# A Fourier layer: half-array forward transform, output in parts of 64 channels

## The chip, the cores and the metric

The kernel runs on one core of one Trainium2 chip. The metric is the device time of one execution in microseconds, as the median of several runs. A core has a matrix engine (TensorE, PE in the profile, with its weight loads as PEld), three elementwise engines (VectorE as DVE, ScalarE as ACT, GpSimd as POOL) and a queue from which transfers are issued (SyncE, SP). Each engine works through its own list of instructions in order, and waits at an instruction until what it needs is there.

## The reference

Four layers follow each other on a tensor of 4 batches, 96 channels and 4096 tokens: a state-space layer, a convolution layer, an attention layer with a quantized feed-forward part, and a Fourier layer with a second such feed-forward part. The change is in the Fourier layer alone:

```
h = einsum('bnc,hc->bnh', layernorm(t), w1)            # 96 -> 192 channels
h = relu(bn(h, bn1...))
X = fft(h, axis=1, norm='ortho')                       # over the 4096 tokens, per channel
xr = relu(X.real * rd - X.imag * id + rb)              # rd, id: one number per channel
xi = relu(X.imag * rd + X.real * id + ib)
y = ifft(xr + 1j * xi, axis=1, norm='ortho').real
t = t + bn(einsum('bnh,ch->bnc', y, w2), bn2...)       # 192 -> 96 channels
```

## The kernel before

A transform over 4096 tokens is done as 128 x 32: token = 32 a + n. The real input is transformed over a (128 points, of which frequencies 0 to 64 are kept), turned by twiddle factors, transformed over the 32 values of n, treated by the ReLU part, and brought back in the opposite order. Everything is float32; a matmul is recorded as two instructions, which the profile counts separately.

The unit of work is an iteration `j` of the loop in `fourier`: a group of G = 6 times 4 channels. There are 32 iterations, 8 per batch; four make one half (96 of the 192 channels) of a batch. The order of instructions on PE, DVE, ACT and POOL is written by hand (`manual_schedule`: program order is queue order), and it is a software pipeline. The transfers on SP are ordered by the scheduler. One iteration `j` emits, in this order:

- `over_n1(j)`: six matmuls over 128 points into `s_ps` (L1390); two DVE products `p` with the twiddles (L1394); two POOL additions that make the real and the imaginary part `f` on 128 partitions (L1402).
- `norm1`, `norm2` (layer norm of the next batch, in iterations where the half is even, for three batches) or `w1`, called by `turn` (the first projection of the next batch, in iterations where the half is odd). `norm1` needs a `misc` buffer on PE, a DVE instruction writes `h` (L1357), ACT squares it; `norm2` is a matmul, two ACT instructions and a POOL product (L1367). `w1` is two matmuls and two ACT instructions that write `hh` (L1378).
- `fold(j-2)`: ACT ReLU on half of `av` (L1436), then on DVE in this order `zz`, `z`, `zz`, `z` (L1441, L1444), and an ACT negation of a part of `zz` (L1447). The two `zz` instructions read two tensors that lie in SBUF.
- `over_k1` and `w2` for two blocks of four token columns, of the half that was finished four iterations before: four matmuls of 128 x 96 weights (L1494), an ACT copy `ys` (L1496), one matmul with the second projection (L1505), one DVE addition into `t` (L1509 or L1511).
- `over_n2(j-1)`: four matmuls of 128 x 128 weights and 390 columns (L1411 to L1414), a DVE product `ec` (L1417), twelve ACT instructions into `av` (L1426), a POOL addition and a POOL subtraction (L1429, L1430).
- `over_k2(j-3)`: twelve matmuls (L1459, L1460) into two PSUM buffers, and an ACT copy `bt` of each (L1461).

Every fourth iteration `row64` sends the row of frequency 64 through a small DRAM buffer into `bt`. The PSUM buffers matter: tag `m` (`misc`) has two and serves `norm1`, `norm2`, `w1`, `over_k1`, `w2` and `row64` in turn; tag `i1` has two and serves `over_k2`. The inverse matrix for a block (`gt`, 256 KB) comes from DRAM, with two buffers; near the end the whole matrix is fetched into free `hh` buffers.

The two blocks are called the first and the second block below. The order of the middle of an iteration, shortened:

```python
over_n1(j)
norm1(b, a, sq)                 # or turn(2)
fold(j - 2)
over_k1(*blocks[0], kept)
norm2(a - MB, sq)
over_n2(j - 1)
norm1(b, a + MB, sq)
w2(*blocks[0], kept)
over_k1(*blocks[1], kept)
over_k2(j - 3)
norm2(a, sq)                    # or turn
w2(*blocks[1], kept)
```

Of the kernel before, what the change touches and what calls it, by code (L numbers as in the profile page):

```python
# [9 lines left out]
F32 = mybir.dt.float32  # L10
# [92 lines left out]
class Net:  # L103
# [717 lines left out]
    def consts2(self, wk, small):  # L821
# [28 lines left out]
        self.dft2 = load("dft2", [128, 3 * 128])  # L850
# [54 lines left out]
        self.a_w2 = pool.tile([C, 2, C], F32, name="a_w2s")  # L905
        for half in range(2):
            ps = small(C, C)
            nc.tensor.matmul(ps, araw[:, half * C : (half + 1) * C], gain, start=True, stop=True)
            nc.vector.tensor_copy(self.a_w2[:, half], ps)
# [425 lines left out]
    def fourier(self, dram, t, h):  # L1335
# [3 lines left out]
        units = [(b, half) for b in range(B) for half in range(2)]  # L1339
        its = [(u, g) for u in range(len(units)) for g in range(0, CG, G)]  # L1340
        with ExitStack() as ctx:
# [3 lines left out]
            nbs, bc, bs = (self.dft2[:, k * 128 : (k + 1) * 128] for k in range(3))  # L1345
# [23 lines left out]
            def w1(b, n):  # L1369

                if n == 0:
                    for half in range(2):
                        hh[2 * b + half] = wk.tile([N1, CG, N2, 4], F32, name="hh", tag="hh", bufs=3)
                ps = misc(N1)[:, : 4 * C].rearrange("p (n c) -> p n c", n=2)
                for d in range(2):
                    nc.tensor.matmul(ps[:, d, :], h[:, n + d :: N2], self.a_w1, start=True, stop=True)  # L1376
                for half in range(2):
                    nc.scalar.activation(  # L1378
                        hh[2 * b + half][:, :, n : n + 2, :].rearrange("p g n c -> p n g c"),
                        ps[:, :, half * C : (half + 1) * C].rearrange("p n (g c) -> p n g c", c=4),  # L1380
                        AF.Relu,
                    )

            def over_n1(i):

                u, g = its[i]
                ps = pln.tile([128, 2, MB], F32, name="s1_ps", tag="s1")
                for d in range(G):
                    a = d % 3 * 2 * K1
                    nc.tensor.matmul(ps[:, d // 3, a : a + 2 * K1], hh[u][:, g + d], self.dft1, start=True, stop=True)  # L1390
                pp = []
                for k in range(2):
                    p = wk.tile([128, G, 2, K1], F32, name=f"p{k}", tag=f"p{k}")
                    nc.vector.tensor_mul(  # L1394
                        p.rearrange("p (a g) r k -> p a g (r k)", a=2),
                        ps[:, :, : 6 * K1].rearrange("p a (g k) -> p a g k", g=3),
                        self.twid[:, k : k + 1, None, :].to_broadcast([128, 2, 3, 2 * K1]),
                    )
                    pp.append(p)
                f[i] = wk.tile([128, 2, G, K1], F32, name="f", tag="f", bufs=2)  # L1400
                for r in range(2):
                    nc.gpsimd.tensor_add(f[i][:, r], pp[0][:, :, r, :], pp[1][:, :, 1 - r, :])  # L1402

            def over_n2(i):

                u, g = its[i]
                cg = units[u][1] * CG + g
                fr, fi = (f[i][:, r].rearrange("p g k -> p (g k)") for r in range(2))
                f.pop(i)
                xr, xi = (pln.tile([128, MB], F32, name=f"x{r}_ps", tag=f"x{r}")[:, : G * K1] for r in "ri")  # L1410
                nc.tensor.matmul(xi, bc, fi, start=True, stop=False)  # L1411
                nc.tensor.matmul(xi, nbs, fr, start=False, stop=True)
                nc.tensor.matmul(xr, bc, fr, start=True, stop=False)
                nc.tensor.matmul(xr, bs, fi, start=False, stop=True)  # L1414
# [17 lines left out]
            def fold(i):  # L1432

                u, g = its[i]
                v = av.pop(i)
                nc.scalar.activation(v[:, 1:3], v[:, 1:3], AF.Relu)  # L1436
                z = zz[i] = wk.tile([128, G, 3, K1 - 1], F32, name="zz", tag="zz", bufs=2)
                if g == 0:
                    z64[u] = wk.tile([128, 2, CG], F32, name="z64", tag="z64", bufs=2)
                for k, (one, two, op) in enumerate(((0, 2, ALU.add), (3, 1, ALU.subtract))):  # L1440
                    nc.vector.scalar_tensor_tensor(  # L1441
                        z[:, :, 1 + k], v[:, one, :, : K1 - 1], 0.0, v[:, two, :, : K1 - 1], ALU.max, op
                    )
                    nc.vector.scalar_tensor_tensor(  # L1444
                        z64[u][:, k, g : g + G], v[:, one, :, K1 - 1], 0.0, v[:, two, :, K1 - 1], ALU.max, op
                    )
                nc.scalar.mul(z[:, :, 0], z[:, :, 2], -1.0)  # L1447

            def over_k2(i):

                u, g = its[i]
                z = zz.pop(i)
                if g == 0:
                    bt[u] = wk.tile([N1, N2, C], F32, name="bt", tag="bt", bufs=2)
                for e in range(0, G, 3):
                    ps = pln.tile([N1, 4, 128], F32, name="i1_ps", tag="i1", bufs=2)[:, :3]
                    for d in range(3):
# [3 lines left out]
                    nc.scalar.copy(  # L1461
                        bt[u].rearrange("p n (g c) -> p g n c", c=4)[:, g + e : g + e + 3],
                        ps.rearrange("p g (n c) -> p g n c", c=4),
                    )

            def row64(u):
                ps = misc(CG)[:, :128]
                for k in range(2):
                    nc.tensor.matmul(ps, z64[u][:, k], self.dft64[:, k], start=k == 0, stop=k == 1)
                r = wk.tile([CG, N2, 4], F32, name="r64", tag="r64", bufs=2)  # L1470
                nc.scalar.copy(r, ps.rearrange("p (n c) -> p n c", c=4))
                d = dram.tile([1, N2 * C], F32, name="d64", tag="d64", bufs=2)
                nc.sync.dma_start(d.rearrange("o (n g c) -> g (o n) c", n=N2, c=4), r)
                nc.sync.dma_start(bt[u][64:65].rearrange("p n c -> p (n c)"), d)
# [3 lines left out]
            def fetch(k):  # L1478

                g = wk.tile([N1, CG, N2, 4], F32, name="hh", tag="hh", bufs=3)  # L1480
                g = g.rearrange("p g n c -> p (g n c)")[:, : N2 // 2 * N1].rearrange("p (n a) -> p n a", n=N2 // 2)
# [4 lines left out]
            def over_k1(u, n, kept):  # L1486
                if n in late:
                    gt = late[n]
                else:
                    gt = wk.tile([N1, 4, N1], F32, name="gt", tag="gt", bufs=2)  # L1490
                    nc.sync.dma_start(gt, ins["idft"][:, n : n + 4])
                ps = misc(C).rearrange("p (n a) -> p n a", n=4)
                for d in range(4):
                    nc.tensor.matmul(ps[:, d], bt[u][:, n + d], gt[:, d], start=True, stop=True)  # L1494
                kept[u, n] = wk.tile([C, MB], F32, name="ys", tag="ys", bufs=2)
                nc.scalar.copy(kept[u, n], ps.rearrange("p n a -> p (n a)"))  # L1496

            def w2(u, n, kept):

                b, half = units[u]  # L1500
                if u < len(units) - 1:
                    ps = misc(C)
                else:
                    ps = pln.tile([N1, 4, 128], F32, name="i1_ps", tag="i1", bufs=2)[:C].rearrange("p n a -> p (n a)")
                nc.tensor.matmul(ps, self.a_w2[:, half, :], kept.pop((u, n)), start=True, stop=True)  # L1505
                ps = ps.rearrange("p (n a) -> p n a", n=4)
                td = ft[b][:, n : n + 4]
                if half == 0:
                    nc.vector.scalar_tensor_tensor(td, ps, self.b2, td, ALU.add, ALU.add)  # L1509
                else:  # L1510
                    nc.vector.tensor_add(td, td, ps)  # L1511

            engines = {mybir.EngineType.PE, mybir.EngineType.DVE, mybir.EngineType.Activation, mybir.EngineType.Pool}
            with tc.manual_schedule(engines=engines):
# [3 lines left out]
                for j in range(len(its) + 4):  # L1518
                    ub, k = divmod(j - 2 * PER, PER)
                    blocks = [(ub, n) for n in (8 * k, 8 * k + 4)] if 0 <= ub < len(units) else []  # L1520
# [30 lines left out]
                    if blocks:  # L1551
                        w2(*blocks[0], kept)
                        over_k1(*blocks[1], kept)
# [6 lines left out]
                    if (j - 6) % PER == 0 and 0 <= (j - 6) // PER < len(units):  # L1560
                        row64((j - 6) // PER)
                    turn(len(tokens))
                    if blocks:
# [4 lines left out]
                last = [(len(units) - 1, n) for n in range(0, N2, 4)]  # L1568
# [31 lines left out]
def _constants():  # L1600
# [9 lines left out]
    th = 2 * np.pi * np.outer(np.repeat(np.arange(N2), 4), k1) / L  # L1610
# [4 lines left out]
    eye = np.eye(4)  # L1615
    bc, bs = np.kron(np.cos(th), eye), np.kron(np.sin(th), eye)
    dft2 = np.concatenate([-bs, bc, bs], 1)

    th = np.pi * np.outer(2 * m + 1, m) / N2
    dft64 = np.stack([np.kron(np.cos(th), eye), np.kron(-np.sin(th), eye)], 1)  # L1620
# [12 lines left out]
        "dft2": dft2.astype(f32),  # L1633
        "dft64": dft64.astype(f32),
# [18 lines left out]
def _lay_out(i):  # L1653
# [20 lines left out]
    for k, v in (("rd", np.diagonal(a["r"])), ("id", np.diagonal(a["i"])), ("rb", a["rb"]), ("ib", a["ib"])):  # L1674
        v128[k] = np.tile(v.reshape(48, 4).T, (32, 1))
# [56 lines left out]
```

## Time and profile before

| what | value |
|---|---|
| median of 3 runs | 3710.8 us (3705.59 to 3724.08) |
| profiled execution, its own time | 3723.78 us |
| span of the profiled execution | 3722.0 us |
| mean granted TensorE clock | 0.914 |
| PE, DVE, ACT, POOL busy | 83%, 81%, 73%, 69% |
| Fourier loop, first `over_n1` to the next layer's first matmul | 3097.04 to 3589.5 us of the span |

Times are microseconds from the start of the span. A group line gives the line of the kernel, the engine, the output and inputs, the shape (partitions x elements), the count, then busy time and mean ns of one, then idle time of the engine before these instructions and what ended it. Overlapping matmuls are recorded with their pipeline, so the mean of one matmul is longer than the step from one to the next. A window line gives, for a stretch of time, the busy time of each engine with the number of instructions.

### The profile page before, as it was taken

The numbers are of one execution on the slowest core, as the hardware profiler recorded it, in microseconds if no ns is written. First come the engines' busy times: TensorE is split into PE (matmuls) and PEld (weight loads), VectorE is DVE, ScalarE is ACT, GpSimd is POOL, SyncE is SP. The second block draws the span as 40 slices with busy tenths as digits, with TensorE's granted clock in tenths as the row PEclk, the third lists the DMA queues.
The fourth block names the chain that finished last, engine by engine and source line by source line (L and its number), as shares of the span: only waits on it lengthen the run. The fifth ranks groups of instructions, "written<-read, shape, count | busy, mean of one in ns | idle before, by whom it ended". The sixth has DMA issues, their size and how long they took to land. (4 is left out here: it accounts for less than half of the span.)

```text
span 3722.0 us, 47365 instructions
## 1 busy us (share of the span) xinstructions
PE 3098.0 (83%) x15360; PEld 1409.3 (38%) x15360; DVE 3020.9 (81%) x2966; ACT 2722.6 (73%) x5584; POOL 2567.9 (69%) x925
## 2 busy tenths in 40 slices
PE   7888788878887888888888878659798888999888
PEld 3332223222322232223222322228345436667643
DVE  5999999999999999999999999962665693444649
ACT  5888888887888887888888878641346786656557
POOL 1989988899899988998998999832001263444427
PEclk8999999989999999899999999859899998999989
DMA  7666656665666666666666666557000000011001
GB/s 186 151 162 155 170 152 161 156 169 153 160 155 169 160 153 156 172 158 152 158 171 160 148 165 160 145 149 272 12 0 1 1 1 6 24 35 47 24 12 58
DMA packets 171552, 446.36 MB, mean 120 GB/s; under 512 B 48756, under 2 KB 50750, under 8 KB 167968
## 3 DMA queue, kind: packets, MB, share of 16 engines
q1 hardware_dynamic: 171304, 443.34, 46.2%
q8 instruction: 121, 1.98, 0.2%
q14 instruction: 127, 1.04, 0.1%
HBM read 369.68 MB, written 73.50 MB: 119 GB/s over the span
## 5 line engine op out<-in xcount | busy, mean ns | idle before, releaser
L648 POOL TENSOR_TENSOR hs<-hs,crep 128x2048 f32<-128x2048 f32 x384 | 1601.7, 4187 | 224.4 <-DVE hs L643 177.2
L610 ACT ACTIVATE da<-ddb,nega 128x1024 f32<-128x1024 f32 x576 | 660.1, 1146 | 200.3 <-DMA ddb<-dd 129.1
L643 DVE TENSOR_TENSOR_SCAN hs<-da,state,rep 128x1024 f32<-128x1024 f32 x288 | 669.5, 2338 | 47.8 <-PE rep L594 28.0
L621 POOL TENSOR_TENSOR up<-udb,brep 128x1024 f32<-128x1024 f32 x192 | 453.6, 2363 | 83.3 <-DMA udb<-ud 62.2
L665 PE MATMUL y<-hs,sel_r 128*32 128x512 f32 x3072 | 462.2, 696 | 12.2 <-POOL hs L648 11.9
L599 PE MATMUL rep<-dbl,sel_b 32*128 32x512 f32 x768 | 249.9, 729 | 215.6 <-DVE hs L643 215.5
L507 ACT ACTIVATE uta<-delta,bt 128x192 f32<-128x192 f32 x1024 | 379.7, 441 | 0.0
L287 PE MATMUL ps<-n,w_x 97*64 97x512 f32 x1536 | 354.5, 604 | 12.5 <-ACT xc L411 11.8
L643 DVE TENSOR_TENSOR_SCAN hs<-da,state,u 128x1024 f32<-128x1024 f32 x144 | 338.1, 2348 | 23.7 <-PE y L665 7.8
L643 DVE TENSOR_TENSOR_SCAN hs<-dap,state,up 128x1024 f32<-128x1024 f32 x144 | 335.3, 2328 | 1.5 <-ACT dap L610 1.4
L594 PE MATMUL rep<-ident,uta 128*128 128x128 f32 x1536 | 223.0, 287 | 103.6 <-DVE hs L643 89.9
L594 PEld LDWEIGHTS rep<-ident,uta 128*128 128x128 f32 x1536 | 175.2, 146 | 248.6 <-issue 136.2
L636 DVE TENSOR_TENSOR u<-udb,rep 128x1024 f32<-128x1024 f32 x192 | 235.3, 1226 | 25.0 <-DMA udb<-ud 11.4
L643 DVE TENSOR_TENSOR_SCAN hs<-da,rep 128x1024 f32<-128x1024 f32 x96 | 218.0, 2281 | 19.5 <-PE rep L594 13.5
L610 ACT ACTIVATE dap<-ddb,nega 128x1024 f32<-128x1024 f32 x192 | 214.1, 1115 | 24.8 <-DVE hs L643 24.3
L636 DVE TENSOR_TENSOR rep<-udb,rep 128x1024 f32<-128x1024 f32 x192 | 231.8, 1207 | 0.0
L1290 POOL CAST hq<-y 128x1536 fp8e5<-128x1536 f16 x64 | 94.0, 1469 | 198.2 <-DVE y L1289 136.3
L287 PEld LDWEIGHTS ps<-n,w_x 97*64 97x64 f32 x1536 | 105.1, 137 | 259.1 <-issue 208.8
L665 PEld LDWEIGHTS y<-hs,sel_r 128*32 128x32 f32 x3072 | 73.9, 119 | 337.1 <-issue 261.7
L599 PEld LDWEIGHTS rep<-dbl,sel_b 32*128 32x128 f32 x768 | 65.8, 205 | 353.5 <-issue 299.1
L658 PE MATMUL y<-xc,dp 128*128 128x512 f32 x192 | 132.0, 778 | 31.3 <-ACT bt L463 31.3
L1157 POOL MEMSET h<- 1x4096 f32 x1 | 3.5, 3507 | 215.0 <-ACT g L1039 215.0
(287 smaller groups left out, 6291.6 us busy)
## 6 DMA issues: line engine op xcount, KB each, us to landing
udb<-ud SPq DMA_DIRECT2D x768, 128.0 KB
ddb<-dd SPq DMA_DIRECT2D x768, 128.0 KB
crep<-cd SPq DMA_DIRECT2D x512, 128.0 KB
dd<-delta SPq DMA_DIRECT2D x64, 384.0 KB
band<-in_band SPq DMA_DIRECT2D x24, 1024.0 KB
ud<-delta SPq DMA_DIRECT2D x62, 384.0 KB
brep<-cd SPq DMA_DIRECT2D x128, 128.0 KB
x<-in_x SPq DMA_DIRECT2D x32, 384.0 KB
```

What stands on the lines that cost most here:

```text
L287: nc.tensor.matmul(ps[rows], w[:, 64 * p : 64 * p + 64], rhs[:, at.start + shift : at.stop + shift], start=k == 0, stop=k == len(ws) - 1, ...
L507: nc.scalar.mul(m["uta"][:, q, :, 32 * s4 : 32 * s4 + 32].rearrange("t (p j) d -> t p j d", p=3), m["udt"][:, :, q].rearrange("t p (j d) - ...
L594: nc.tensor.transpose(x[:, q * 128 : q * 128 + 128], made[k]["uta"][:, q, 2 * h + j], self.ident)
L599: nc.tensor.matmul(x[:, at], sel_b[rows, g], made[k]["dbl"][rows, at], start=True, stop=True)
L610: nc.scalar.activation(da, made[k]["dd", h, j], AF.Exp, scale=nega[:, col : col + 1])
L621: nc.gpsimd.tensor_mul(up, made[k]["ud", p][:, j], made[k]["brep", GP])
L636: nc.vector.tensor_mul(u, made[k]["ud", h][:, j], x)
L643: nc.vector.tensor_tensor_scan(hs[:, 1:], made[k].pop(("da", t)), u, st, ALU.mult, ALU.add)
L648: nc.gpsimd.tensor_mul(hs[:, :, :T], hs[:, :, 1:], twice(made[k]["crep", g]))
L658: nc.tensor.matmul(y, dp[:, items[k][2], p], made[k]["xc"][:, p], start=True, stop=True)
L665: nc.tensor.matmul(made[k]["y", p][row : row + 32], sel_r, made[k]["hs", p, g][:, j, at], start=False, stop=True, skip_group_check=True,)
L1290: nc.gpsimd.tensor_copy(q, y2, saturate=False)
```

## The change

The forward transform over 32 points is laid out differently. The partitions of `s_ps` now hold (channel, n) in place of (n, channel), and `f` holds, for two of the four channels at a time, the real part on partitions 0 to 63 and the imaginary part on 64 to 127. Each of the four matmuls of `over_n2` then needs no accumulation and has 64 output columns; the two halves `q` write the two halves of the partitions. `f` is made by four POOL additions of 64 partitions, where there were two of 128; two of the four read one half of the partitions and write the other. `hh` has the token index innermost, so `w1` writes it with a step of 32 elements.

The output side works on thirds of 64 channels in place of halves of 96. A block has eight token columns: the four matmul pairs of `over_k1` put four of them on partitions 0 to 63 and four on 64 to 127, a single ACT copy `ys` takes both, and `w2` is two matmuls of 64 contraction rows into two PSUM buffers, with a DVE addition for each. There are 48 such blocks where there were 64. `w2` takes its PSUM from tag `i1`, which `over_k2` uses too, and no longer from `m`. Each block needs two `gt` tiles. Blocks are done two or one in an iteration, by a list. `row64` runs 12 times with 16 rows, in place of 8 times with 24.

```diff
-                        hh[2 * b + half] = wk.tile([N1, CG, N2, 4], F32, name="hh", tag="hh", bufs=3)
+                        hh[2 * b + half] = wk.tile([N1, CG, 4, N2], F32, name="hh", tag="hh", bufs=3)
...
                     nc.scalar.activation(
-                        hh[2 * b + half][:, :, n : n + 2, :].rearrange("p g n c -> p n g c"),
-                        ps[:, :, half * C : (half + 1) * C].rearrange("p n (g c) -> p n g c", c=4),
+                        hh[2 * b + half][:, :, :, n : n + 2].rearrange("p g c n -> p n (g c)"),
+                        ps[:, :, half * C : (half + 1) * C],
                         AF.Relu,
...
-                for r in range(2):
-                    nc.gpsimd.tensor_add(f[i][:, r], pp[0][:, :, r, :], pp[1][:, :, 1 - r, :])
+                for q, rows in enumerate(parts):
+                    for r in range(2):
+                        nc.gpsimd.tensor_add(f[i][parts[r], q], pp[0][rows, :, r, :], pp[1][rows, :, 1 - r, :])
...
-                nc.tensor.matmul(xi, bc, fi, start=True, stop=False)
-                nc.tensor.matmul(xi, nbs, fr, start=False, stop=True)
-                nc.tensor.matmul(xr, bc, fr, start=True, stop=False)
-                nc.tensor.matmul(xr, bs, fi, start=False, stop=True)
+                for r, x in ((1, xi), (0, xr)):
+                    for q, rows in enumerate(parts):
+                        nc.tensor.matmul(
+                            x[rows], self.dft2[:, r], fs[:, q], start=True, stop=True, skip_group_check=True
+                        )
...
             def over_k1(u, n, kept):
-                ps = misc(C).rearrange("p (n a) -> p n a", n=4)
+                ps = misc(128).rearrange("p (n a) -> p n a", n=4)
                 for d in range(4):
-                    nc.tensor.matmul(ps[:, d], bt[u][:, n + d], gt[:, d], start=True, stop=True)
+                    for q, rows in enumerate(parts):
+                        nc.tensor.matmul(
+                            ps[rows, d],
+                            bt[u][:, n + 4 * q + d],
+                            gts[q][:, d],
...
             def w2(u, n, kept):
-                nc.tensor.matmul(ps, self.a_w2[:, half, :], kept.pop((u, n)), start=True, stop=True)
-                ps = ps.rearrange("p (n a) -> p n a", n=4)
-                td = ft[b][:, n : n + 4]
+                ps = [pln.tile([N1, MB], F32, name="i_ps", tag="i1", bufs=2)[:C] for _ in range(2)]
+                for p, rows in zip(ps, parts):
+                    nc.tensor.matmul(p, self.a_w2[rows, third], y[rows], start=True, stop=True)
+                for q, p in enumerate(ps):
+                    p = p.rearrange("p (n a) -> p n a", n=4)
+                    td = ft[b][:, n + 4 * q : n + 4 * q + 4]
...
+            todo, ready = [], [(8 * b + r, b * U + q) for b in range(B) for q, r in enumerate((5, 8, 10))]
...
-                    ub, k = divmod(j - 2 * PER, PER)
-                    blocks = [(ub, n) for n in (8 * k, 8 * k + 4)] if 0 <= ub < len(units) else []
+                    todo += [(u, n) for r, u in ready if r + 2 == j for n in range(0, N2, 8)]
+                    many = (2, 1, 2, 2, 1, 1, 2, 1)[j % 8]
+                    blocks, todo = todo[:many], todo[many:]
```

## The prediction, made before the changed kernel ran

> **What bounds the kernel now.** I read the slices first: until about 2500 us the core is in layer 0, where the change does nothing. The stages of the Fourier loop come next, read in windows cut at the starts of `over_n1`: iterations 8 to 11 (with `norm1` and `norm2`), 12 to 15 (with `w1`), and 24 to 31 (neither).
>
> ```profile
> core 0: us, PE busy (x) PEld busy (x) DVE busy (x) ACT busy (x) POOL busy (x), PEclk, DMA share, GB/s
> 3191.72:3254.06 62.34, 58.87 (x294) 38.05 (x295) 30.64 (x44) 39.77 (x96) 32.17 (x25) 0.97 0.13 35
> 3254.06:3316.97 62.91, 57.24 (x327) 46.49 (x326) 27.78 (x35) 36.80 (x107) 24.43 (x18) 1.00 0.12 35
> 3442.48:3536.53 94.05, 84.25 (x521) 63.65 (x520) 61.80 (x72) 54.21 (x146) 47.24 (x32) 1.00 0.09 24
> ```
>
> PE is about 90% busy, DMA idle. This looks like a PE bound, and the change takes PE work away. Whether that pays is decided by what PE would wait for next, so I read the timeline of one iteration, started on PE at 3206.45 and followed by the next at 3221.69 (15.24 us):
>
> ```profile
> 3208.40 1.85 DVE L1394 TENSOR_TENSOR p<-s_ps,twid 128x780 f32<-128x780 f32 x2 [0.49 <-PE s_ps L1390]
> 3210.39 1.87 POOL L1402 TENSOR_TENSOR f<-p,p 128x390 f32<-128x390 f32 x2 [1.60 <-DVE p L1394]
> 3211.41 0.84 ACT L1436 ACTIVATE av<-av 128x780 f32<-128x780 f32 x1
> 3212.28 0.56 DVE L1441 SCALAR_TENSOR_TENSOR zz<-av 128x384 f32<-128x384 f32 x1 [1.44 <-ACT av L1436]
> 3213.42 0.52 ACT L1447 ACTIVATE zz<-zz 128x384 f32<-128x384 f32 x1 [1.17 <-DVE zz L1441]
> 3213.85 0.56 ACT L1496 COPY ys<-m_ps 96x512 f32<-96x512 f32 x1
> 3214.47 1.10 PE L1356 MATMUL m_ps<-t,ones 96*96 96x512 f32 x2
> ```
>
> In time order a second chain runs beside PE: `p` on DVE, ReLU on ACT, `zz` on DVE, negation and `ys` on ACT. The second `norm1` needs the buffer that `ys` frees, and starts 0.06 us after it (3214.47, `ys` over at 3214.41), though the four `over_n2` matmuls (2.62 us) had only just let PE go. The two chains are level: shortening PE alone gains nothing. Iterations 12 to 15 and 24 to 31 already wait 0.7 and 1.2 us on `ys` before `w2`.
>
> The last row to know is what GpSimd does to `zz`:
>
> ```profile
> 3256.55 1.28 POOL L1367 TENSOR_TENSOR h<-h,ln_rs 96x512 f32<-96x512 f32 x1 [1.46 <-ACT ln_rs L1366]
> 3257.32 2.73 DVE L1441 SCALAR_TENSOR_TENSOR zz<-av 128x384 f32<-128x384 f32 x1
> 3257.78 1.85 POOL L1402 TENSOR_TENSOR f<-p,p 128x390 f32<-128x390 f32 x2
> 3259.97 0.15 DVE L1444 SCALAR_TENSOR_TENSOR z<-av 128x6 f32<-128x6 f32 x1
> ```
>
> `zz` takes 0.55 us alone and 2.73 us here: it ends 0.4 us after the second `f`. In iterations 24 to 31 even the six-element `z` takes 0.85 to 0.98 us and the pair of `f` 2.44 in place of 1.87. A DVE instruction with two SBUF inputs and a POOL addition exclude each other, and the waiting one gets in after one POOL instruction, at worst after all that are queued.
>
> **Part by part: costs**
>
> ```profile
> L1402 POOL TENSOR_TENSOR f<-p,p 128x390 f32<-128x390 f32 x64 | 65.2, 1039 | 97.4 <-DVE p L1394 94.6 <-PE m_ps L1376 2.8
> L1509 DVE SCALAR_TENSOR_TENSOR t<-m_ps,bn_b,t 96x512 f32<-96x512 f32 x32 | 39.0, 1220 | 73.9 <-PE m_ps L1505 73.9
> L949 ACT COPY xt<-xt_ps 128x384 f32<-128x384 f32 x16 | 12.6, 788 | 3.3 <-PE xt_ps L943 3.3
> 2520.10 1.03 POOL L967 COPY x<-xt 64x1024 f32<-64x1024 f32 x1 [55.86 <-DVE xt L947]
> 2521.17 1.04 POOL L968 COPY x<-xt 64x1024 f32<-64x1024 f32 x1
> ```
>
> *`over_n2`.* Four matmuls at 0.655 us become two pairs side by side. In layer 0 a pair with 64 columns and 512 wide steps by 1.01 us where one 128-column matmul takes 0.86, so 1.3 to 1.55 us in place of 2.62: at most 1.3 us off PE, 42 us over 32 iterations.
>
> *`over_k1`, `w2`.* A block cost 0.88 + 0.86 us of PE; the new one about 0.95 + 0.95 (row pairs in layer 0: twelve instructions in 2.82 us, 0.94 a pair). 64 blocks become 48: about 20 us off PE. ACT loses 16 `ys` copies (9 us). But DVE has 96 additions of 1.2 us for 64: two behind each block.
>
> *`f`.* Four additions of 64 partitions. L967 and L968 copy 64 partitions each, on different halves; 1024 elements took 1.04 us, against 1.47 for 1536 on 128 partitions, and the second began when the first was over. So time goes by elements per partition: 4 x 0.93 in place of 2 x 0.93 (the unobstructed pair, 1.87). The rows that move to other partitions have no example; I bound them by 0.47 (half, if partitions counted) and 1.9 (double) and take 0.93.
>
> A rule here speaks against my reading. The Trainium skill (GPSIMD Engine Reference, 2.1 Instruction dispatch) says that consecutive Pool instructions are no barrier between its cores, each serving 16 partitions and starting the next instruction as soon as its own share is done. By it two additions on different halves could overlap, and the sum would be near the second rival's. The L967/L968 rows show no overlap.
>
> *`hh`.* The strided row L949 costs 788 ns for 384 elements, `bt` with runs of four 510 ns. So the 331 ns of `hh` (192 elements) may rise to about 0.48: two more pairs ahead of the ReLU, about 0.5 us an iteration with `w1`. Before the loop PE (0.91 us a `w1`) covers it.
>
> *`i1` buffers.* New wait: the first `over_k2` matmul waits for the first addition of the first block, the seventh for the second; the second `w2` waits for both `bt` copies.
>
> *Others.* Eight more `bt` pieces and four more `row64` lie beside waits. `gt` needs two tiles between blocks: a load issued at 3209.72 had moved its bytes by 3212.1, two take some 3.5 us, and 5 us or more lie between blocks; without that cover 1 us a block. On SP, `row64` stands ahead only of `gt` loads that wait for PE anyway.
>
> **The walk.** Start of `over_n1` = 0, second-block additions of the iteration before pending.
>
> *With norm, two blocks.* Additions 0.2 to 2.65; `p` to 4.55 (before: 3.8); `h` to 5.15; square and ReLU to 6.6. Four `f` from 4.7, of which `zz` waits through the third, the second `zz` through the fourth: it ends at 9.55 (before: 6.95). Negation and `ys` 10.55 (7.9); `norm1` 11.55; `w2` 12.55; first addition 13.95; `over_k2` 14.1 to 16.8; `norm2` 17.7; `w2` 18.7. Instead of 15.24. After a one-block iteration 17.9; with one block 17.7. The four (2, 1, 2, 2): 17.9 + 17.7 + 17.9 + 18.7 = 72.2 against 61.5, the mean of 62.34 and 60.66. Twice: **+21**. The 1.3 us from `over_n2` lie inside PE's wait.
>
> *With `w1`* (14.65 now): `zz` 1 us later, `over_k2` 0.6 us later: 16.4 with two blocks, 15.5 with one. For 1, 1, 2, 1: +4.3, with `hh` +6.3. Twice: **+12.6**.
>
> *Iterations 24 to 31* (11.58 now): the circle is `w2`, addition, `p`, `zz`, negation, `ys`, `w2`, `over_k2`, `w2`. Two blocks about +1.7, one about +0.2 (four of each): **+7**. Another circle, twelve `av` (3.6), two POOL (3.7), ReLU, `zz`, negation, `ys`, sums to 11 us: less than that cannot come.
>
> *Iterations 0 to 7*: no additions, one block, but `zz` behind `f` in the circle of `av`, about 1 us in six, and `hh`: **+7**.
>
> *Tail* after iteration 32: eleven blocks for 16, at two additions (2.45 us) each: **-5.5**.
>
> Sum +42 on the profiled 3723.78, so 3766; that execution lies 13 us above the median, and the forecast is 3710.8 + 42 = **3753**.
>
> **Rivals.** Second, *`f` costs as before*, or `zz` always passes first: then `zz` is late by the additions alone. Norm +1.4 and +0.5, about +9; `w1` about +2; last iterations +5; tail -5.5: **+11, 3722**. The contended rows above speak against it.
>
> Third, faster: *PE is the bound after all.* The place is the second `norm1`: if `ys` came before PE reaches it, then the time of an iteration is PE's list, less 2.2 us of its 13.6, plus about 1 us for the changes between array shapes (0.15 us each by the layer 0 pair): 28 iterations at about -1.1, about **-30, 3681**. It decides if `ys` comes within 6.7 us of `over_n1`; today it is 7.9, and only earlier `zz` could do it.
>
> On those changes of shape the Trainium skill (TensorEngine Tiling (Array Packing), Key Properties) says that a change of tiling mode drains the array; no row isolates one.
>
> Fourth, *POOL keeps the port*: `zz` waits for all four `f`, as in the 2.73 us row, or the moved rows cost double. Another 1.9 us in iterations with `w1`, 2.8 in the last eight, 2 in the early ones: +50, so **+92, 3803**.
>
> **Numbers.** Forecast 0.55, fourth 0.22, second 0.14, third 0.09. Below 0.5% (18.6 us), about what a measurement can tell from no change, lies the second alone. Faster 0.09, same 0.14, slower 0.77. The range 3704 to 3800 leaves out the third and half of the fourth.
>
> **What would show it.** Right: `f` x128 at about 0.93 to 1.2 us; PE idle before the second `norm1` on `ys`, about 3 us an iteration; `zz` means well over 758 ns; `i_ps` matmuls waiting for DVE `t`; norm iterations of about 18 us. Wrong: PE still 90% busy in the loop, or `f` at half its time.

## The result, and the profile after

The changed kernel takes 3757.95 us, median of four runs (3752.44 to 3762.86), against 3717.44 us before, median of four: a ratio of 1.0109, 95% interval 1.0085 to 1.0133. It is slower by 1.1%, and the forecast was 3753. The total came out as predicted; the experiments show that its largest part did not come from where the prediction put it.

The profiled execution took 3752.44 us (3723.78 before). The stages of the Fourier loop, cut at the starts of `over_n1` as for the kernel before: iterations 8 to 11, 12 to 15, and 24 to 30. In the windows of the changed kernel:

```profile
core 0: us, PE busy (x) PEld busy (x) DVE busy (x) ACT busy (x) POOL busy (x), PEclk, DMA share, GB/s
3186.36:3253.79 67.43, 54.42 (x357) 30.75 (x358) 40.83 (x49) 39.99 (x97) 40.16 (x31) 1.00 0.19 56
3253.79:3322.57 68.78, 55.81 (x346) 44.76 (x344) 35.16 (x40) 39.99 (x105) 34.18 (x26) 0.88 0.13 39
3457.42:3551.95 94.53, 73.33 (x541) 51.69 (x541) 58.43 (x70) 48.26 (x130) 55.89 (x42) 0.91 0.12 35
```

PE is busy for about 80% where it was 90%. What is new is the granted clock (`PEclk`): in the iterations with `w1` (second line) and in the last ones it is 0.88 and 0.91, where the windows shown of before had 1.00. In the iterations with `norm` it is 1.00 (0.97 before).

| Stage (iterations) | before, us | after, us | difference |
|---|---|---|---|
| 1 to 7 | 88.81 | 94.31 | +5.5 |
| with `norm`, 8 to 11 and 16 to 19 | 62.18 + 60.82 | 67.43 + 67.51 | +11.9 |
| with `w1`, 12 to 15 and 20 to 23 | 62.91 + 64.85 | 68.78 + 67.34 | +8.4 |
| 24 to 30 | 82.47 | 94.53 | +12.1 |
| 31 and tail, to the next layer | 64.56 | 65.13 | +0.6 |

Two of the prediction's cuts lie 0.16 us behind the start of `over_n1`, so it read 62.34 and 60.66 for 62.18 and 60.82; the sum is the same. The stages together, from the second `over_n1` to the next layer's first matmul, take 486.6 us before and 525.0 after: +38.4. I call this stretch "the loop" below. (The two profiled executions differ by less, 28.7 us, since the layers ahead of the loop were done 10.9 us earlier in the changed kernel's.) Groups of the changed kernel between 3080 and 3620 us (busy time, mean ns of one, then idle time ahead and what ended it):

```profile
L1414 POOL TENSOR_TENSOR f<-p,p 64x390 f32<-64x390 f32 x128 | 137.7, 1076 | 133.3 <-DVE p L1405 121.9 <-PE xr_ps L1423 4.7
L1468 PE MATMUL i_ps<-idft,zz 128*128 128x128 f32 x384 | 89.2, 319 | 17.6 <-DVE t L1535 11.5 <-DVE t L1537 6.1
L1530 PE MATMUL i_ps<-ys,a_w2s 64*96 64x512 f32 x192 | 62.1, 676 | 54.0 <-ACT ys L1522 52.3 <-DVE t L1537 1.7
L1455 DVE SCALAR_TENSOR_TENSOR z<-av 128x6 f32<-128x6 f32 x64 | 54.2, 847 | 0.0
L1388 ACT ACTIVATE hh<-m_ps 128x192 f32<-128x192 f32 x109 | 45.8, 541 | 23.2 <-PE m_ps L1386 22.7
L1452 DVE SCALAR_TENSOR_TENSOR zz<-av 128x384 f32<-128x384 f32 x64 | 39.9, 624 | 39.3 <-ACT av L1447 39.3
```

The same instructions in the kernel before, `over_k2`, `w2`, `zz` and `z`:

```profile
L1459 PE MATMUL i_ps<-dft,zz 128*128 128x128 f32 x384 | 76.7, 282 | 0.0
L1505 PE MATMUL m_ps<-ys,a_w2s 96*96 96x512 f32 x112 | 60.3, 620 | 28.8 <-ACT ys L1496 28.2 <-ACT ln_rs L1365 0.6
L1441 DVE SCALAR_TENSOR_TENSOR zz<-av 128x384 f32<-128x384 f32 x64 | 48.5, 758 | 33.4 <-ACT av L1436 33.4
L1444 DVE SCALAR_TENSOR_TENSOR z<-av 128x6 f32<-128x6 f32 x64 | 24.7, 386 | 0.0
```

In the changed kernel's list the first line is the four `f` as forecast: 128 of 1076 ns, no overlap. The second has the new wait of `over_k2` for the additions that free `i1`: 17.6 us, where the same matmuls waited for nothing before. The third has PE's wait for `ys` ahead of `w2`: 52.3 us, 28.2 before. The fourth and sixth show that `zz` itself got cheaper (624 ns, 758 before) and the six-element `z` dearer (847, 386 before): DVE gets in between two POOL instructions, and `z` is then held by the next. In a `norm` iteration of 18.03 us the timeline reads:

```profile
3239.95 4.58 POOL L1414 TENSOR_TENSOR f<-p,p 64x390 f32<-64x390 f32 x4 [2.90 <-DVE p L1405]
3241.84 0.56 DVE L1452 SCALAR_TENSOR_TENSOR zz<-av 128x384 f32<-128x384 f32 x1 [1.44 <-ACT av L1447]
3242.32 0.85 DVE L1455 SCALAR_TENSOR_TENSOR z<-av 128x6 f32<-128x6 f32 x1
3243.09 0.55 DVE L1452 SCALAR_TENSOR_TENSOR zz<-av 128x384 f32<-128x384 f32 x1
3243.67 0.52 ACT L1458 ACTIVATE zz<-zz 128x384 f32<-128x384 f32 x1 [1.86 <-DVE zz L1452]
3244.10 0.57 ACT L1522 COPY ys<-m_ps 128x512 f32<-128x512 f32 x1
3244.72 1.10 PE L1366 MATMUL m_ps<-t,ones 96*96 96x512 f32 x2 [1.70 <-ACT ys L1522]
```

This is the chain that the prediction walked: `zz`, negation, `ys`, second `norm1`. From the iteration's start at 3235.76 the second `zz` ends after 7.9 us (6.95 was read before, 9.55 forecast), and PE waits 1.70 us (about 3 forecast).

### The profile page after: what moved, and what is told of

The parts are those of the page before. It is cut to its first block, busy times and chain, and to the rows that moved or that the text cites. A ratio compares the mean times of both kernels' runs of the same rounds, so it can differ in the third digit from the quotient of the medians.

```text
span 3750.7 us, 48164 instructions
## 1 busy us (share of the span) xinstructions
PE 3076.1 (82%) x15704; PEld 1379.6 (37%) x15704; DVE 3071.4 (82%) x2999; ACT 2735.7 (73%) x5580; POOL 2641.2 (70%) x989
## 5 line engine op out<-in xcount | busy, mean ns | idle before, releaser
L665 PE MATMUL y<-hs,sel_r 128*32 128x512 f32 x3072 | 460.1, 693 | 12.7 <-POOL hs L648 11.9
L1414 POOL TENSOR_TENSOR f<-p,p 64x390 f32<-64x390 f32 x128 | 137.7, 1076 | 133.3 <-DVE p L1405 121.9
L1405 DVE TENSOR_TENSOR p<-s_ps,twid 128x780 f32<-128x780 f32 x64 | 59.1, 965 | 128.8 <-issue 66.6
```

Source lines behind the costliest of these rows:

```text
L665: nc.tensor.matmul(made[k]["y", p][row : row + 32], sel_r, made[k]["hs", p, g][:, j, at], start=False, stop=True, skip_group_check=True,)
L1414: nc.gpsimd.tensor_add(f[i][parts[r], q], pp[0][rows, :, r, :], pp[1][rows, :, 1 - r, :])
```

## The experiments

All twelve in one table, each from one profile for the loop and from 3 or 5 rounds for the ratio. The loop leaves out the layers ahead of it, which are the same in all and put its start anywhere between 3091 and 3106 us. But it rests on one execution each, and how much a loop differs from one execution to the next was not measured. Where the clock is 1.00 the same work repeats within 0.1 us (67.43 and 67.51 above); where it is not, the two groups with `w1` of the kernel before differ by 1.9 us. The ratios have intervals of 4 to 10 us to each side, and by them most runs lie up to 10 us further from before than by the loop (`a_fwd_alone` +41 for +31.7, `b_last_alone` +19 for +10.1). A difference of a few us between two loops shows little by itself. The clock is the granted one in the loop.

| Run | loop, us | against before | clock | ratio to before (95%) |
|---|---|---|---|---|
| before | 486.6 | | 0.97 | |
| after | 525.0 | +38.4 | 0.92 | 1.0109 (1.0085–1.0133) |
| a_fwd_alone | 518.3 | +31.7 | 0.92 | 1.0111 (1.0087–1.0135) |
| b_last_alone | 496.7 | +10.1 | 0.97 | 1.0051 (1.0034–1.0068) |
| e1_two_f | 517.9 | +31.3 | 0.91 | 1.0095 (1.0071–1.0119) |
| e5_n2_twice | 507.8 | +21.2 | 0.97 | 1.0075 (1.0055–1.0095) |
| e6_before_n2_half | 506.6 | +20.0 | 0.92 | 1.0055 (1.0033–1.0076) |
| e2_one_add | 520.5 | +33.9 | 0.91 | 1.0115 (1.0089–1.0141) |
| e3_hh_dense | 525.0 | +38.4 | 0.92 | 1.0116 (1.0089–1.0143) |
| b_defer | 528.3 | +41.7 | 0.94 | 1.0123 (1.0098–1.0148) |
| e7_twice_two_f | 497.7 | +11.1 | 0.98 | 1.0032 (1.0018–1.0047) |
| e8_twice_one_add | 503.8 | +17.2 | 0.97 | 1.0053 (1.0037–1.0069) |
| c_last_split | 487.1 | +0.5 | 0.98 | 0.9999 (0.9987–1.0011) |
| c_after_split_twice | 496.9 | +10.3 | 0.99 | 1.0034 (1.0020–1.0049) |

**The two halves of the change.** `a_fwd_alone` puts the new `over_n1`, `over_n2`, `hh` order and constants into the kernel before; `b_last_alone` puts the old ones into the changed kernel.

> The kernel before with the first half of the change alone: the forward transform on half arrays (four f of 64 partitions, pairs in over_n2, hh and the constants in the new order); the last transform and the projection as before. Theory (zz waits behind twice as many POOL instructions, hh costs more on ACT): this part carries most of the loss, +25 to +35 us against before, and PE's wait ahead of the second norm1 grows though over_n2 is 1.3 us shorter. Rival 1 (the doubled additions behind w2 carry the loss): within 8 us of before. Rival 2 (PE is the bound, the loss is all in the other half): -30 us.

> The second half of the change alone: thirds of 64 channels, token blocks side by side, two additions behind each block; forward transform, hh and constants as before. Theory: +5 to +15 us against before (norm +9, last iterations +5, tail -5.5). Rival 1 (additions carry the loss): +25 to +40. Rival 2 (fewer PE instructions pay): -20.

The loops give +31.7 and +10.1 us, together 41.8 where the change has 38.4. The forward half carries three quarters of the loss, as the theory said, though it is the half that takes 42 us off PE. (By the ratios the halves add up to 60 us where the change has 40, so the shares are rougher than the decimals.)

**Is it `f` on POOL?** The theory's main term, taken out:

```
-                for q, rows in enumerate(parts):
-                    for r in range(2):
-                        nc.gpsimd.tensor_add(f[i][parts[r], q], pp[0][rows, :, r, :], pp[1][rows, :, 1 - r, :])
+                for r in range(2):
+                    nc.gpsimd.tensor_add(f[i][:, r], pp[0][:, :, r, :], pp[1][:, :, 1 - r, :])
```

> The changed kernel with f by two additions of 128 partitions, as before, in place of four of 64 (the values stand on other partitions than over_n2 needs: the reordering is left out; hh stays strided, over_n2 stays in pairs). Theory (the POOL time of f and what waits on it is the cause): 25 to 31 us less than the changed kernel, +11 to +16 against before; zz and z return to about 760 and 390 ns or less. Rival (the additions and i1, hh, or the clock): at most 10 us less than the changed kernel, +30 or more against before.

The loop fell by 7.2 us (525.0 to 517.9), not by 25 to 31. The theory fell here: with `f` as cheap as before, four fifths of the loss stood, at a clock of 0.91.

**What is PE's time worth?** Twice the same question, from both sides. `e5_n2_twice` gives the changed kernel the 1.3 us an iteration of PE time back; `e6_before_n2_half` takes it from the kernel before and touches nothing else.

```
e5:
-                for r, x in ((1, xi), (0, xr)):
+                for r, x in ((1, xi), (0, xr), (1, xi), (0, xr)):
e6:
-                nc.tensor.matmul(xi, bc, fi, start=True, stop=False)
-                nc.tensor.matmul(xi, nbs, fr, start=False, stop=True)
-                nc.tensor.matmul(xr, bc, fr, start=True, stop=False)
-                nc.tensor.matmul(xr, bs, fi, start=False, stop=True)
+                nc.tensor.matmul(xi, bc, fi, start=True, stop=True)
+                nc.tensor.matmul(xr, bc, fr, start=True, stop=True)
```

> The changed kernel with every over_n2 matmul issued twice (the second writes the same values): 32 x 1.3 = 42 us more PE work, where the change had taken 42 us away. Theory (over_n2 lies inside PE's wait): within 6 us of the changed kernel, +35 to +47 against before. Rival (PE sets the time of an iteration): 30 to 42 us more than the changed kernel, about +80 against before. If the clock of PE falls after long waits and this keeps it busier, a little faster than the changed kernel is possible.

> The kernel before with two of the four over_n2 matmuls of each iteration (the two that accumulate are left out): PE loses 1.3 us an iteration, as in the change, and no other engine's work changes. Theory (the second chain and PE are level, PE's time here is worth nothing): within 6 us of before. Rival 1 (PE bounds the loop): 30 to 42 us less. Rival 2 (longer waits of PE cost clock, as the run with over_n2 twice suggests): 5 to 20 us more than before, with a granted clock under 0.95 in the iterations with w1 and the last eight.

Both theories lost; what came is what the last sentence of the first text and the second rival of the second allowed for, a cost in clock. With 42 us more PE work the loop is 17.3 us shorter, and with 42 us less it is 20.0 us longer. The stages speak for the clock: from the changed kernel to `e5` the `norm` iterations, at 1.00 in both, stay as they are (67.43 and 67.51 to 67.42 and 67.47), while those with `w1` (to 63.54 and 61.90, at 0.97 and 1.00) and 24 to 30 (to 89.07, at 0.98) give 16.1 of the 17.3. Iterations 1 to 7 gain next to nothing (94.31 to 94.16), though their clock rises from 0.89 to 0.93. In `e6` iterations 16 to 19, at 1.00, stay (60.81), and 24 to 30, at 0.89, take 92.39 for 82.47. Where it goes shows in one of the last iterations. The PE timeline of the kernel before:

```profile
3504.61 0.82 PE L1413 MATMUL xr_ps<-f,dft 128*128 128x390 f32 x2
3505.26 0.82 PE L1414 MATMUL xr_ps<-f,dft 128*128 128x390 f32 x2
3507.31 1.10 PE L1505 MATMUL m_ps<-ys,a_w2s 96*96 96x512 f32 x2 [1.22 <-ACT ys L1496]
3508.24 1.04 PE L1494 MATMUL m_ps<-hh,bt 128*96 128x128 f32 x8
```

and of `e6_before_n2_half`, the same place:

```profile
3500.33 0.82 PE L1412 MATMUL xr_ps<-f,dft 128*128 128x390 f32 x2
3503.68 1.10 PE L1503 MATMUL m_ps<-ys,a_w2s 96*96 96x512 f32 x2 [2.54 <-ACT ys L1494]
3504.62 1.86 PE L1492 MATMUL m_ps<-hh,bt 128*96 128x128 f32 x8
```

`ys` comes when it did, so the wait grows by the 1.3 us saved, from 1.22 to 2.54. Then the four matmuls of `over_k1` (x8, two instructions each) take 1.86 us in place of 1.04. The windows of that kernel, cut at the edges of the slow stretch:

```profile
3501.25:3504.67 3.42, 0.99 (x3) 0.46 (x4) 3.14 (x5) 2.03 (x6) 2.23 (x2) 1.00 0.00 0
3504.67:3508.08 3.41, 3.41 (x18) 3.41 (x17) 1.14 (x1) 2.97 (x10) 0.84 (x1) 0.50 0.00 0
3508.08:3511.49 3.41, 3.41 (x27) 2.90 (x27) 0.61 (x1) 1.43 (x3) 2.83 (x2) 1.00 0.02 5
```

In the 3.42 us with the wait PE was busy for 0.99 us; then the granted clock is 0.50 for exactly 3.41 us, and 1.00 after that. So the 1.3 us saved go into the wait, and the slow stretch comes on top: the iteration takes 13.2 us where it took 11.6. In the changed kernel, where the wait ahead of `w2` is 2.39 us:

```profile
3486.83:3490.24 3.41, 1.36 (x10) 0.32 (x6) 3.41 (x6) 0.71 (x2) 2.22 (x2) 1.00 0.00 0
3490.24:3493.65 3.41, 3.07 (x14) 1.52 (x16) 2.05 (x4) 3.41 (x13) 2.04 (x3) 0.50 0.00 0
3493.65:3497.07 3.42, 3.42 (x34) 3.13 (x32) 1.17 (x2) 1.52 (x5) 2.76 (x2) 1.00 0.00 0
```

The Trainium skill (TensorE: Matmul & The Clock Gate, Part 1: The HAM clock gate) describes this gate: windows of about 3.4 us that run freely, half clock after an idle one, full clock after a busy one. The lengths here agree with it. The section HAM oscillation of the same page puts the rule as no idle gaps above about 3.4 us; there the measurements differ, since waits of 2.39 and 2.54 us, in windows with 1.36 and 0.99 us of PE work, were enough. With `over_n2` twice the same wait of the changed kernel is 1.08 us, and those iterations run at 0.98:

```profile
3491.87 1.10 PE L1530 MATMUL i_ps<-ys,a_w2s 64*96 64x512 f32 x4 [1.08 <-ACT ys L1522]
```

It also matters where a wait falls. Iterations 24 and 26 of the changed kernel have the same wait, and only the second is followed by a slow `w2`:

```profile
3463.74 1.10 PE L1530 MATMUL i_ps<-ys,a_w2s 64*96 64x512 f32 x4 [2.39 <-ACT ys L1522]
3490.58 2.02 PE L1530 MATMUL i_ps<-ys,a_w2s 64*96 64x512 f32 x4 [2.39 <-ACT ys L1522]
```

All edges of slow stretches in a profile lie on one grid of 3.413 us, within 2 ns. On this grid the wait of iteration 24 is split between two windows, with 1.84 and 2.33 us of PE work; that of iteration 26 lies in the one window shown above, with 1.36 us.

```profile
3459.52:3462.93 3.41, 1.84 (x18) 0.79 (x14) 3.41 (x6) 0.23 (x1) 1.75 (x2) 1.00 0.50 147
3462.93:3466.35 3.42, 2.33 (x21) 1.31 (x22) 2.99 (x4) 3.42 (x12) 2.52 (x3) 1.00 0.04 11
```

The loops of the fourteen profiles have 1838 such windows at full clock. Where PE was busy for less than 40% of a window, the next one ran at half clock in 93 of 93 cases; at 40 to 50% in 57 of 80, at 50 to 60% in 16 of 89, at 60 to 80% in 6 of 386, and above that in none of 1190.

**The other suspects.** `e2_one_add` leaves out the second addition behind each `w2`; `e3_hh_dense` writes `hh` in runs of four as before.

```
e2:
-                for q, p in enumerate(ps):
+                for q, p in enumerate(ps[:1]):
e3 (the order of the access pattern alone):
-                        hh[2 * b + half][:, :, :, n : n + 2].rearrange("p g c n -> p n (g c)"),
+                        hh[2 * b + half].rearrange("p g c n -> p g (c n)").rearrange("p g (n c) -> p g n c", c=4)[:, :, n : n + 2].rearrange("p g n c -> p n g c"),
```

> The changed kernel without the second of the two additions behind each w2 (half of the last layer's output is not added to t): 48 additions of 1.2 us less. Theory (the additions stand ahead of p and in the circle of the last iterations): 20 to 28 us less than the changed kernel, of it about 7 in the sixteen norm iterations each way, 5 in the last eight and 12 in the tail after iteration 32. Rival (they lie beside PE's waits on ys): only the tail's 12.

> The changed kernel with hh written in runs of four as before (the values stand in another order than the constants expect: the reordering is left out). hh returns to about 331 ns. Theory (hh alone matters little, the wait on zz is as long): 2 to 6 us less than the changed kernel, in the iterations with w1. Rival (hh is what the iterations with w1 lost): 8 to 12 us less, and their clock back at 1.00.

Half of the additions gone gave 4.5 us, and the stretch from iteration 31 on alone gave 5.5 (65.1 to 59.7 us): the rival was right about the place, though not about the 12 us. `hh` went back from 541 to 340 ns, and the loop stayed at 525.0:

```profile
L1388 ACT ACTIVATE hh<-m_ps 128x192 f32<-128x192 f32 x112 | 30.7, 340 | 34.9 <-PE m_ps L1386 34.9
```

Two shifts cancel in that. The iterations with `w1` took 3.0 us less (65.98 and 67.12 for 68.78 and 67.34), as the theory had it, and iterations 8 to 11 took 71.11 for 67.43, at a clock of 0.93. The rival is out, since the clock in the `w1` iterations stayed at 0.92 and 0.90; what `hh` is worth, some 3 us or nothing, one profile with a moving clock does not settle.

**Moving the additions.** In the second half alone, a `w2`'s additions are kept back until the next iteration's `p` are issued:

```
-                        w2(*blocks[1], kept)
+                        w2(*blocks[1], kept, adds)
...
                         over_n1(j)
+                    while adds:
+                        adds.pop()()
```

> The run of the second half of the change alone, with one thing moved: the additions of an iteration's second block come on DVE behind the next iteration's two p in place of ahead of them. All values are computed. Theory (the doubled additions cost by holding back p, and with it f and zz): norm iterations return from 64.7 to about 60 us for four, the last seven from 87.4 to about 82, so 12 to 20 us less than the second half alone and within 8 us of before. Rival (the i1 buffers or w2 hold, not p): no change against the second half alone, +18 against before.

It cost 31.6 us more than `b_last_alone` (528.3 against 496.7), a miss in sign. In iteration 17 `p` begins 1.7 us after `over_n1`, and 2.4 without the move: only 0.7 earlier, since it needs `over_n1`'s output first. The additions had run while DVE waited for that output. Now they stand between `p` and `h`, which begins at 5.6 in place of 4.1, and in other iterations ahead of `zz`. PE waits 2.7 to 2.9 us for `h` or `ys`, and the clock is 0.94.

**The terms again, with the clock held.** Since the clock covered the other terms, two of them were measured once more on top of `e5_n2_twice`: `f` by two additions, and one addition per `w2` less (the edits shown above).

> The changed kernel with over_n2 issued twice and with f by two additions of 128 partitions (the reordering of partitions is left out): the cost of the four f with PE's clock held. Theory (the clock was the larger part of the loss; f costs about 0.6 us in each norm iteration): 4 to 10 us less than the run with over_n2 twice alone, and the half-rate stretches stay rare, +20 to +25 us against before. Rival (f is the main term, as the prediction had it, and was hidden in the earlier run by the clock): 25 to 31 us less, level with before.

> The changed kernel with over_n2 issued twice and the second addition behind each w2 left out (half of the last layer's output is not added): the cost of the doubled additions with PE's clock held. Theory: 12 to 20 us less than the run with over_n2 twice alone (about 6 in the eight norm iterations, 5 in the last eight, 5 in the tail), +10 to +17 against before. Rival (the additions lie beside the wait on zz): 5 us less, the tail alone.

Against 507.8, the four `f` are worth 10.1 us (to 497.7), about 2.1 us in every four `norm` iterations and 2.5 in the mean of the four with `w1`. The doubled additions are worth 4.0 (to 503.8), 3.4 of it behind iteration 30. So for `f` the theory's 4 to 10 us held at its upper end (its +20 to +25 against before did not: +11.1), and for the additions the rival. In `e7` the clock was not held everywhere: iterations 24 to 30 took 90.45 for 89.07, at 0.96.

**The buffers of `w2`.** What remained was the 17.6 us wait of `over_k2` for `i1`. The two outputs of a `w2` are put into different pools:

```
-                ps = [pln.tile([N1, MB], F32, name="i_ps", tag="i1", bufs=2)[:C] for _ in range(2)]
+                ps = [misc(C), pln.tile([N1, MB], F32, name="i_ps", tag="i1", bufs=2)[:C]]
```

> The second half of the change alone, with one thing changed: the two outputs of a w2 lie one in the m buffers and one in i1, in place of both in i1. All values are computed. Theory (over_k2 waits 1.2 to 1.3 us for the addition that frees i1, in fourteen iterations, and this wait goes): 8 to 18 us less than the second half alone, 0 to +10 against before. Rival (the wait moves to the m buffers, or PE idles elsewhere): within 5 us of the second half alone, +13 to +20 against before.

> The changed kernel with both remedies: over_n2 issued twice, and the two outputs of a w2 in an m and an i1 buffer. All values are computed. Theory: 8 to 16 us less than the run with over_n2 twice alone, +12 to +20 against before, so better than the change and still not better than before. Rival (PE is now full enough for the extra matmuls to count): no gain over the run with over_n2 twice.

Both theories held: 9.6 us less than `b_last_alone`, and 10.9 less than `e5_n2_twice` (though +10.3 against before, where +12 to +20 was expected). In the groups the wait of `over_k2` is 18.4 us in `b_last_alone` (first line) and 9.3 in `c_last_split` (second), and there PE's wait for `ys` (third, 21.2) is below the 28.2 of the kernel before:

```profile
L1466 PE MATMUL i_ps<-dft,zz 128*128 128x128 f32 x384 | 80.2, 292 | 18.4 <-DVE t L1533 11.4 <-DVE t L1535 7.0
L1466 PE MATMUL i_ps<-dft,zz 128*128 128x128 f32 x384 | 79.5, 289 | 9.3 <-DVE t L1533 6.1 <-DVE t L1535 3.1
L1528 PE MATMUL m_ps<-ys,a_w2s 64*96 64x512 f32 x96 | 52.3, 627 | 22.7 <-ACT ys L1520 21.2 <-ACT ln_rs L1374 1.1 <-DVE t L1535 0.4
```

`c_last_split`, the second half with this remedy and without the forward half, is level with the kernel before (0.9999, 0.9987 to 1.0011). No version here beats it.

## Why the prediction was right, and where it was not

The forecast was +42; the medians show +40.5 and the loop +38.4. Its division by parts held as well, by the loops: "`f` costs as before" was priced at +11, which leaves 31 to the forward half, and the two halves measure +10.1 and +31.7. But the 31 is not what the prediction said it was. Taking remedies one at a time from the changed kernel's 38.4: PE's time and clock 17.3 (`e5`), then, on top of it, the wait for `i1` 10.9 (`c_after_split_twice`) and the four `f` 10.1 (`e7`). These add up to 38.3; that they do add was not tried in one kernel with all three.

Step by step:

- *`over_n2`, PE's time inside a wait, worth nothing.* The duration was right (two pairs in 1.31 us). The value was wrong, and it is the step that failed: worth nothing to the chain, the shorter PE work lengthens PE's wait and costs clock, 20.0 us in the kernel before (`e6`).
- *`f` and `zz`, the main term.* 1076 ns each, no overlap: right. The price was too high: 10.1 us with the clock held, 7.2 without, where the walk had about 31. The second `zz` ended at 7.9 us, not 9.55, because it came in between two `f` and not behind the last; the sign that "`zz` means well over 758" was wrong (624), and `z` paid in its place; PE's idle time ahead of the second `norm1` is 1.7 us, not about 3.
- *The `norm` iterations*, +21: measured +11.9, at full clock. With `f` by two additions and the clock held they still stand at 65.4 for four (62.18 and 60.82 before).
- *The `w1` iterations*, +12.6, of it 4 for `hh`: measured +8.4, and with the clock held -2.3 (63.54 and 61.90 for 62.91 and 64.85), `hh` still strided. So what they lost goes with the clock; `hh` alone moved them by 3.0 in `e3`, and the loop by nothing.
- *Iterations 24 to 31*, +7 (its own terms add up to 7.6): measured +12.1 for seven; 5.5 of it returns with the clock.
- *Iterations 0 to 7*, +7: measured +5.5. Little can be said of its cause: in the kernels with the old forward half and the new last half, whose early iterations hardly differ, the stage took 90.7 to 93.9 us, against 88.81 before and 94.3 here.
- *The tail*, -5.5: measured +0.6. The additions' time (`e2`: 5.5 less) and the buffers (`c_last_split`: 59.6 for 64.6 before) stood in the way; with the buffers apart the expected gain is there.
- *`i1`.* Right in kind (`over_k2` waits on `t`), and about 10 us.

Oversized terms for `f` and `norm` thus stood in for a term that was missing: the cost of the half-rate clock stands nowhere in the sum. That the sum came within 4 us of the loop is luck to that extent; the sign, the doubled `f` and the wait for `i1` are not. That the third rival is out is shown directly: PE is not the bound, since less of its work made the loop longer. The second rival, +11 by the additions alone, is what the loop costs once the clock and `f` are removed (`e7`: +11.1), and by `c_last_split` most of it is the buffers, not the additions. The fourth did not occur: `zz` did not wait for all four `f`.

Open: at 40 to 80% of busy time a window was followed by full clock in some cases and by half in others, and what decides there is not known. That the place of a wait on the grid matters is read from the profiles; it was not tested by moving one.

## What to carry to other kernels

Before work is taken off an engine that waits anyway, ask how long the wait becomes: on TensorE a wait that grew from 1.2 to 2.5 us, by just the time that was saved, made an iteration 1.6 us longer through the clock, and the granted clock by stage is the column that shows it. Where a clock effect is in play, measure an edit's parts again with the clock held, since it covers their real sizes. When outputs are doubled, look who else uses their buffers: here one PSUM tag cost 10 us, more than twice what the doubled additions themselves did.

## What was not expected of the hardware

- Half-rate stretches, whole multiples of 3.41 us long, can follow waits of PE of 2.4 to 2.5 us, though PE was busy for 40% of the window ahead (1.36 of 3.41 us). The same wait, split between two windows, cost no clock.
- Adding 42 us of matmuls that change no value made the changed kernel's loop 17.3 us shorter.
- A six-element DVE instruction beside POOL additions takes 847 ns in the mean, 414 where POOL has half as many instructions (`e7_twice_two_f`), though a 384-element one beside it takes 624.
- An ACT write of 192 elements to single, strided places takes 541 ns, and 340 in runs of four.
